# Half products of the layer 1 attention in two steps, the expert plan in two parts, row loads behind the last relay

## The chip, the cores and the metric

The kernel runs on one core of a Trainium2 chip. The metric is the device time of one execution in microseconds (us); for the kernel before, three runs are given, and their median counts.

## The reference, cut to what matters

Everything is float32. x has 8 images of 256 channels and 32 x 32 places, so 8 batches of 1024 tokens of 256 numbers.

```python
# layer 0, for each batch: xt is (1024, 256); 8 heads of 64
qkv = (xt @ w_qkv + b_qkv).reshape(B, S, 8, 192)
q, k, v = jnp.split(qkv, 3, axis=-1)
attn = softmax(jnp.einsum('bihd,bjhd->bijh', q, k) * SCALE, axis=1)   # over the queries i
res = jnp.einsum('bijh,bjhd->bihd', attn, v).reshape(B, S, 512)
t = res @ w_out + b_out + xt
# layer 1: attention of the normed tokens with themselves
n = layer_norm(t)
scores = jnp.einsum('bne,bme->bnm', jnp.einsum('bnd,ed->bne', n, W), n)
t = t + jnp.einsum('bnm,bmd->bnd', softmax(scores, axis=-1), n)
# experts: for each token the two of 8 that its router scores highest
n = layer_norm(t)
t = t + sum_e(combine_e * (gelu(n @ w1[e] + b1[e]) @ w2[e] + b2[e])) + n   # out starts from the tokens n
```

The softmax of layer 0 runs over the queries. With the keys as rows of a tile, each row is therefore a softmax of its own, and its sum divides the row of values.

## The kernel before, in words

One program goes through the batches in turn. Batch b has a layer 0, then the layer 1 attention (`attend`), then a norm, the routing and the sending of its normed tokens to rows in HBM, sorted by expert (`rows`, scattered by GpSimd). After the last layer 0 the experts of the batches sent until then run over 63 blocks of these rows; then come the attention of batch 7 and its experts, done densely. Each engine takes its instructions in the order in which the scheduler has laid them; `tc.issue_after(x)` in the code says that what follows is to be laid behind instruction x on the same engine, and makes no wait between engines.

**Layer 0** (`layer0`, from line 465) takes 4 pairs of heads g times 8 blocks of keys j, 32 steps. A step computes scores `psc` on TensorE (`score`, line 492, two tiles of 128 keys x 1024 queries), their maximum on VectorE in two halves (`first_max`, line 507; `second_max`, line 516, which writes `scrap` and the maximum), the exponential with its sum on ScalarE (`soften`, line 533), the division of the values by the sum on VectorE (`divide`, `vs`, line 549), and, two steps later, the products with the values `po` on TensorE (`gather_values`, line 569). TensorE is kept from starting a half of these products before the last half by an empty instruction, the relay (line 579): it waits for the products of one half, and those of a half in the next turn wait for it. For batch 0 the relay stands in GpSimd's queue, for the others in SyncE's.

At three steps, `PROJECT` = (0,3), (1,1), (2,1), sixteen products of the projection of the next pair (`pqk`, line 371, 7.06 us together) fill TensorE, while the maxima of that step have been taken. Work for VectorE is laid into this time: the counts and places of the routing of the batch before (`share`), and at (2,1) the residual (`residual`, lines 454 to 462): two transposes of the input tile on VectorE and an addition of the bias on GpSimd.

In the last layer 0 (b = 7), at (2,1) and behind the residual, stands the plan (`plan`, lines 1092 to 1166). It is some thirty small VectorE instructions that turn the counts of rows for each expert into a list: for each block of 256 rows the expert that it belongs to, its first row (`row_at`) and the place of the expert's weights (`w_at`). Two kinds of instruction wait for the list. GpSimd gathers the weights of the first blocks (`weights`, line 1222), by `w_at`. SyncE loads rows (`fetch`): it reads `row_at` into a register (`value_load`, line 1234) and issues the four loads of a block (`xr`, line 1239); before the change the first of them is laid behind nothing. VectorE then transposes the rows (`xb`, line 1245), and the first products of the experts (`ph`, line 1256), gelu (`hb`, line 1266) and second products (`pe`, line 1282) follow.

After the last `po`, layer 0 ends with the output product `pr` (line 666, 64 matmuls), which VectorE adds to the residual.

**Layer 1** (`attend`, from line 673) norms the tokens, projects them (`px`, line 703) and computes scores of 1024 x 1024 as four pairs of blocks of 128 rows. A pair (`Pair`) makes its two blocks in seven half products (line 753) instead of eight, from sums of halves that VectorE makes beforehand (t1 to t4, s1 to s4). The product x lies in one bank of an accumulator and grows: ScalarE copies it after its first product (line 741, `first`), after its second (line 745, `second`) and after its third (line 748), into tiles `home` (their name in the trace is `home` or `spare`); VectorE adds other products to these copies, taking the minimum on the way (`add`, line 763). `rest` makes the last two products and the exponentials (lines 786, 795, 803). A block is then transposed for the product with the tokens: block 0 and block 7 on TensorE (`turn_now`, line 842), the others (`turn`) by one VectorE transpose of squares (line 824) and sixteen moves of squares (line 835), eight of them copies on ScalarE, eight DMAs of SyncE. `mix` multiplies the turned block with the tokens (`py`, line 852).

The order of it is written by hand at the end of `attend`. In before, `Pair(k)` makes five of the seven products at once, and `rest` the other two.

Of the kernel before, what the change touches and what calls it, by code (L numbers as in the profile page):

```python
# [12 lines left out]
AF = mybir.ActivationFunctionType  # L13
ALU = mybir.AluOpType
# [5 lines left out]
def kernel(  # L20
# [23 lines left out]
    nc = tc.nc  # L44
# [420 lines left out]
    def layer0(b, xT, begun, routing, xs):  # L465
# [91 lines left out]
        def gather_values(at, turn):  # L557
# [7 lines left out]
            for half in range(2):  # L565
                keys = ts(half, DK)
                n = (half + turn) % 2
                for h in range(2):
                    mm = nc.tensor.matmul(  # L569
                        po[n][ts(h, DK), :],  # L570
                        vss[at][keys, h, :],
                        exps[at, h][keys, ts(n, 512)],
                        start=(j == 0 and turn == 0),
                        stop=(j == NT - 1 and turn == 1),
                    )
                    if h == 0 and (j > 0 or turn > 0):
                        tc.add_manual_dep(mm.ins, past[1 - half].ins.name, BEHIND)

                turned[half] = relay.nop()  # L579
                tc.add_manual_dep(turned[half].ins, mm.ins.name, BEHIND)  # L580
# [23 lines left out]
        for at in range(last + LAG + 1):  # L604
# [38 lines left out]
            if at <= last and (g, j) in PROJECT:  # L643
# [4 lines left out]
                if (g, j) == PROJECT[-1]:  # L648
                    with tc.issue_after(firsts[at, 1].ins):
                        t1 = residual(b, xs)  # L650
                if g == 0:
                    with tc.issue_after(mm.ins), tc.issue_after(firsts[at, 1].ins):
                        counted = share(pq)
                if b == B - 1 and (g, j) == PROJECT[-1]:
                    with tc.issue_after(firsts[at, 1].ins):
                        plan(groups[0])
            elif at <= last and (g, j) > PROJECT[1]:
# [15 lines left out]
    def attend(b, t1, fill, tick=nothing):  # L673
# [51 lines left out]
        class Pair:  # L725

            def __init__(self, k):
# [8 lines left out]
                ]  # L736
                left, right = (self.ex[0][:, ts(n, HALF)] for n in range(2))
                far = self.ex[1][:, ts(1, HALF)]
                at = ts(k, P)
                self.product(self.x, a11, b11, True)  # L740
                self.first = nc.scalar.copy(left, self.x)
                second = self.product(v, a12, b21, True)
                tc.declare_no_dep(second.ins, self.first.ins, reason="the other bank")
                self.product(self.x, s2_, t2_, False)
                self.second = nc.scalar.copy(right, self.x)
                self.product(self.z, s1_, t1_, True)
                self.product(self.x, s3_, t3_, False)
                nc.scalar.copy(far, self.x)
                self.add(left, v, 3.0e38, self.low[0])
                self.add(far, self.z, 3.0e38, self.low[1])  # L750

            def product(self, to, stationary, moving, start):
# [20 lines left out]

            def rest(self):
                k = self.k
# [8 lines left out]
                def even():  # L784
                    tick(("max", 2 * k), self.add(ex0[:, HALF:], self.z, self.low[0], nmax[0]))
                    nc.scalar.activation(
                        ex0, ex0, AF.Exp, bias=nmax[0], scale=-1.0, accum_out=ssum[0][:, 0:1]
                    )

# [80 lines left out]

        pairs = [Pair(0), Pair(1)]
        first, second = pairs[0].rest()
        second = turned(*second)
        third, fourth = pairs[1].rest()
        now = turn_now(0, first[1])
        pairs.append(Pair(2))
        third = turned(*third, (pairs[2].first, pairs[2].second))
        fourth = turned(*fourth, (pairs[2].second, pairs[2].second))
        mix(0, now, *first[2:])
        mix(*second)  # L880
        fifth, sixth = pairs[2].rest()
        fifth = turned(*fifth)
        mix(*third)
        pairs.append(Pair(3))
        sixth = turned(*sixth, (pairs[3].second, pairs[3].second))
        mix(*fourth)
# [192 lines left out]
    def plan(group):  # L1079
# [6 lines left out]
        def tmp(tag, shape, dtype=F32):  # L1086
# [39 lines left out]
        nc.vector.tensor_mul(block, block, taking)  # L1126
        nc.vector.tensor_add(block, block, after)

        mine = tmp("p_mine", [nb, E])
# [13 lines left out]

        base = tmp("p_base", [E])
        nc.vector.tensor_scalar_mul(base, first, -float(BR))
        work = tmp("p_work", [nb, E])
# [6 lines left out]
        row_at = keep.tile([P, NBMAX], I32, tag="row_at", name=f"row_at_{n}", bufs=2)  # L1153
        nc.vector.tensor_copy(row_at[:, :nb], lo)
        nc.vector.tensor_scalar(hi, e_of, float(P), p_iota, ALU.mult, ALU.add)
# [7 lines left out]
        w_at = keep.tile([P, NBMAX], I32, tag="w_at", name=f"w_at_{n}", bufs=2)  # L1163
        nc.vector.tensor_copy(w_at[:, :nb], hi)

        nc.vector.tensor_scalar(
            first[:, E // 2 :], first[:, E // 2 :], left, None, ALU.subtract
        )
        group.first = first, turns
        group.where = row_at, w_at  # L1170

    def places(group):
# [40 lines left out]
    def experts(group, behind):  # L1213
# [17 lines left out]
        def fetch(b):  # L1231
            xr = rowp.tile([P, RUN, DQ], F32, tag="xr", name=f"xr_{n}_{b}")
            with tc.issue_after(loads[-1].ins) if loads else nullcontext():
                at = nc.sync.value_load(
# [404 lines left out]
```

## Time and profile before

| | us |
|---|---|
| three runs | 2336.98, 2338.59, 2345.87 |
| median | 2338.59 |
| the profiled execution | 2327.18 |
| its span on the core | 2325.2 |
| TensorE busy | 2259.1 (97%) |
| VectorE busy | 1561.8 (67%) |
| ScalarE busy | 1167.0 (50%) |
| GpSimd busy | 411.2 (18%) |
| mean granted clock of TensorE | 0.993 |

In the lines of the profile, PE is TensorE, PEld its loading of weights, DVE VectorE, ACT ScalarE, POOL GpSimd and SP SyncE; SPq is SyncE's queue, which has no work of its own but instructions and DMAs to issue. A line of a timeline has the start in the span, the duration, the engine, the line of the kernel, the operation, what it writes and reads, the shape and the number of instructions that were merged into it; in brackets stands the idle time ahead of it and what ended it. A line of waits has who waited for what: us in total, times, and the longest. The chain is the work that ended last, followed back through what released it.

Single times from the timeline, for orientation: the first and the last scores (psc) of the last layer 0 start at 1715.19 and 1863.56, of batch 6 at 1474.75 and 1610.09; the projection at its step (2,1) starts at 1794.09 and ends at 1801.15; its first `pr` starts at 1873.40. The attention of batch 1 has its first `px` at 437.38 and its last `py` at 504.05, that of batch 0 at 189.51 and 263.89, that of batch 7 at 2113.22 and 2185.99.

### The profile page before, as it was taken

The numbers are of one execution on the slowest core, as the hardware profiler recorded it, in microseconds if no ns is written. First come the engines' busy times: TensorE is split into PE (matmuls) and PEld (weight loads), VectorE is DVE, ScalarE is ACT, GpSimd is POOL, SyncE is SP. The second block draws the span as 40 slices with busy tenths as digits, with TensorE's granted clock in tenths as the row PEclk, the third lists the DMA queues.
The fourth block names the chain that finished last, engine by engine and source line by source line (L and its number), as shares of the span: only waits on it lengthen the run. The fifth ranks groups of instructions, "written<-read, shape, count | busy, mean of one in ns | idle before, by whom it ended". The sixth has DMA issues, their size and how long they took to land.

```text
span 2325.2 us, 37960 instructions
## 1 busy us (share of the span) xinstructions
PE 2259.1 (97%) x13059; PEld 1211.7 (52%) x13059; DVE 1561.8 (67%) x4029; ACT 1167.0 (50%) x2139; POOL 411.2 (18%) x392
## 2 busy tenths in 40 slices
PE   9999999999999999999999999999999899999798
PEld 3344634563356335643554355435553278886565
DVE  5775678567865786578757775677668756435765
ACT  3664466356635663656464656465546532224311
POOL 0000012000200030003000200021002124544663
PEclk9999999999999999999999999999999999999899
DMA  8995201020102010201020101100120237765664
GB/s 293 385 386 156 69 12 45 4 61 8 49 1 55 12 53 1 46 19 51 6 40 25 44 13 24 41 21 17 19 45 19 71 90 196 194 190 156 189 201 134
DMA packets 278759, 200.10 MB, mean 86 GB/s; under 512 B 189576, under 2 KB 232232, under 8 KB 276776
## 3 DMA queue, kind: packets, MB, share of 16 engines
q1 hardware_dynamic: 252472, 139.14, 21.3%
q0 software_dynamic: 25008, 58.01, 7.8%
q8 instruction: 104, 1.70, 0.3%
q10 hardware_dynamic: 1088, 0.52, 0.1%
q14 instruction: 87, 0.71, 0.1%
HBM read 108.88 MB, written 110.90 MB: 95 GB/s over the span
## 4 chain that ended last, share of the span: by engine, by line
PE 80%; ACT 6%; DVE 5%; DMA 4%; issue 3%; SPq 1%; POOL 0%; DVEq 0%; ACTq 0%; POOLq 0%
PE po L569 19%; PE psc L492 18%; PE pqk L371 7%; PE py L852 6%; PE pr L666 5%; PE pv L408 4%; PE ps L753 3%; PE ph L1256 3%; PE pe L1282 3%; PE pdy L1529 2%; PE pdh L1505 2%; PE px L703 2%; PE pqk L349 2%; DMA y<-yb 1%; ACT aT L835 1%
## 5 line engine op out<-in xcount | busy, mean ns | idle before, releaser
L533 ACT ACTIVATE ex<-psc,nmax 128x1024 f32<-128x1024 f32 x512 | 570.5, 1115 | 309.9 <-DVE scrap L516 225.9
L569 PE MATMUL po<-ex,vs 64*64 64x512 f32 x4096 | 569.6, 593 | 10.7 <-SPq L579 9.8
L492 PE MATMUL psc<-qk,qk 64*64 64x512 f32 x4096 | 573.0, 593 | 3.6 <-ACT ex L533 3.5
L516 DVE TENSOR_SCALAR_CACHE_REDUCE scrap<-psc,nmax 128x512 f32<-128x512 f32 x512 | 384.4, 751 | 166.6 <-PE psc L492 138.7
L507 DVE TENSOR_REDUCE nmax<-psc 128x1 f32<-128x512 f32 x512 | 350.3, 684 | 9.3 <-PE psc L492 9.3
L492 PEld LDWEIGHTS psc<-qk,qk 64*64 64x64 f32 x4096 | 178.7, 132 | 281.1 <-ACT ex L533 131.5
L569 PEld LDWEIGHTS po<-ex,vs 64*64 64x64 f32 x4096 | 173.1, 132 | 287.8 <-issue 84.2
L1070 POOL DMA_INDIRECT rows<-n,d_at x112 | 109.0, 973 | 663.6 <-DVE nmax L507 663.3
L997 POOL TENSOR_TENSOR t<-t,n 128x2048 f32<-128x2048 f32 x8 | 36.3, 4536 | 876.8 <-DVE n L263 876.8
L371 PE MATMUL pqk<-xT,wqkv 128*128 128x512 f32 x384 | 171.2, 599 | 0.0
L336 ACT ACTIVATE qk<-pqk,b_qks 128x512 f32<-128x512 f32 x124 | 85.6, 690 | 86.6 <-PE pqk L371 77.5
L371 PEld LDWEIGHTS pqk<-xT,wqkv 128*128 128x128 f32 x384 | 71.0, 190 | 99.9 <-issue 76.5
L1378 POOL DMA_INDIRECT yk<-y,yat x112 | 111.4, 995 | 60.4 <-issue 25.6
L408 PE MATMUL pv<-wqkv,xT 128*128 128x512 f32 x256 | 120.3, 599 | 1.6 <-DVE v L416 1.0
L852 PE MATMUL py<-n,spare 128*128 128x256 f32 x512 | 118.0, 386 | 3.9 <-DMA out_dram<-oT 3.2
L852 PEld LDWEIGHTS py<-n,spare 128*128 128x128 f32 x512 | 98.3, 193 | 29.0 <-issue 16.4
L666 PE MATMUL pr<-wo,res 128*128 128x256 f32 x512 | 111.9, 379 | 0.0
L835 ACT COPY spare<-home 32x256 f32<-32x256 f32 x256 | 103.0, 402 | 10.1 <-DVE home L824 6.7
L666 PEld LDWEIGHTS pr<-wo,res 128*128 128x128 f32 x512 | 97.2, 190 | 17.0 <-ACT res L588 3.2
L1266 ACT ACTIVATE hb<-ph,wb 128x256 f32<-128x256 f32 x96 | 40.4, 471 | 125.4 <-issue 84.0
L533 ACT ACTIVATION_READ_ACCUMULATOR ex<-psc,nmax 128x1 f32 x512 | 99.1, 194 | 0.0
L1256 PE MATMUL ph<-xb,wb 128*128 128x256 f32 x384 | 91.8, 381 | 5.7 <-DMA wb<-wpack,w_at 4.1
(256 smaller groups left out, 2889.6 us busy)
## 6 DMA issues: line engine op xcount, KB each, us to landing
rows<-wb SPq DMA_DIRECT2D x7, 8192.0 KB
xr<-rows SPq DMA_DIRECT2D x252, 64.0 KB
y<-yb POOLq DMA_DIRECT2D x63, 256.0 KB, 2.6
xs<-in_x_dram SPq DMA_DIRECT2D x64, 128.0 KB
spare<-home SPq DMA_DIRECT2D x256, 32.0 KB
out_dram<-oT SPq DMA_DIRECT2D x60, 128.0 KB
xT<-in_x_dram SPq DMA_DIRECT2D x7, 1024.0 KB
sums<-t SPq DMA_DIRECT2D x7, 1024.0 KB
```

The costliest lines, as they stand in the source:

```text
L371: mm = nc.tensor.matmul(pq[:, ts(n, 512)], wqkv[:, cc, t, ts(g, P)], xT[:, cc, ts(n, 512)], start=(cc == 0), stop=(cc == NCC - 1),)
L408: nc.tensor.matmul(pv, self.xT[:, cc, ts(i, P)], wqkv[:, cc, 2, :], start=(cc == 0), stop=(cc == NCC - 1),)
L492: mm = nc.tensor.matmul(pss[at, h][ts(c, DK), ts(n, 512)], k[r, j * P + c * DK : j * P + (c + 1) * DK], q[r, ts(n, 512)], start=True, stop ...
L507: firsts[at, h] = nc.vector.tensor_reduce(nmax, pss[at, h][:, ts(0, 512)], AX.X, ALU.max, negate=True)
L516: seconds[h] = nc.vector.tensor_scalar(scrap, pss[at, h][:, ts(1, 512)], -1.0, nmaxes[at, h], ALU.mult, ALU.min, accum_out=nmax,)
L533: nc.scalar.activation(ex, pss.pop((at, h)), AF.Exp, bias=nmaxes.pop((at, h)), scale=1.0, accum_out=sums[at][:, h : h + 1],)
L569: mm = nc.tensor.matmul(po[n][ts(h, DK), :], vss[at][keys, h, :], exps[at, h][keys, ts(n, 512)], start=(j == 0 and turn == 0), stop=(j == ...
L666: nc.tensor.matmul(pr[:, :C], res[:, g, ts(i, P)], wo[:, g, :], start=(g == 0), stop=(g == NPAIR - 1))
L835: move(to[ts(k, SQ), a], since[ts(a, SQ), k])
L852: evicted["mixed"] = nc.tensor.matmul(py[:, :D], aT[m], n1[:, m, :], start=(m == 0), stop=(m == NT - 1))
L1256: last = nc.tensor.matmul(ph[:, ts(fc, BR)], wb[:, dc * FF + fc * P : dc * FF + (fc + 1) * P], xb[:, dc, :], start=(dc == 0), stop=(dc == ...
L1378: ins = nc.gpsimd.indirect_dma_start(out=self.slot(at)[:, k, :], out_offset=None, in_=self.group.y[:, :], in_offset=bass.IndirectOffsetOnAxis(
```

## The change

It has three parts.

1. **Half products in two steps a pair.** `Pair(k)` now makes three products (x's first, v and z's first), and its new method `middle` the second and third of x, with their copies. The first two pairs do both at once. Pair 2's `middle` is laid behind the first mix, and pair 3's behind the third; pair 3 itself starts before the third mix. The moves of block 5 (`fifth`) and block 6 (`sixth`) are laid behind copies of pair 3, those of `third` and `fourth` as before behind copies of pair 2. The exponential of the first block is laid behind the third copy of pair 1 (`rest(pairs[1].third)`).
2. **The plan in two parts.** `plan` becomes a generator. Its first part, up to the block numbers, `base` and the rest of `first`, runs at step (1,1) of the last layer 0; its second part, up to `row_at` and `w_at`, at (2,1), ahead of the residual, which is laid behind it.
3. **Row loads behind the last relay.** The first `fetch` is laid behind the last relay of the last layer 0 (`evicted["relayed"]`) on SyncE, so that no row load stands between relays.

```diff
--- before.py
+++ after.py
@@ -576,7 +576,7 @@
                     if h == 0 and (j > 0 or turn > 0):
                         tc.add_manual_dep(mm.ins, past[1 - half].ins.name, BEHIND)
 
-                turned[half] = relay.nop()
+                turned[half] = evicted["relayed"] = relay.nop()
                 tc.add_manual_dep(turned[half].ins, mm.ins.name, BEHIND)
             if turn == 0:
                 return mm
@@ -646,14 +646,19 @@
                     pair, pq, mm = project_pair(b, xT, g + 1)
                 qks.append(pair)
                 if (g, j) == PROJECT[-1]:
-                    with tc.issue_after(firsts[at, 1].ins):
+                    ahead = firsts[at, 1]
+                    if b == B - 1:
+                        with tc.issue_after(ahead.ins):
+                            ahead = next(planning)
+                    with tc.issue_after(ahead.ins):
                         t1 = residual(b, xs)
                 if g == 0:
                     with tc.issue_after(mm.ins), tc.issue_after(firsts[at, 1].ins):
                         counted = share(pq)
-                if b == B - 1 and (g, j) == PROJECT[-1]:
+                if b == B - 1 and (g, j) == PROJECT[1]:
+                    planning = plan(groups[0])
                     with tc.issue_after(firsts[at, 1].ins):
-                        plan(groups[0])
+                        next(planning)
             elif at <= last and (g, j) > PROJECT[1]:
                 share(firsts[at, 1])
         for _ in routing:
@@ -734,20 +739,23 @@
                     small.tile([P, 1], F32, tag=f"nlow{h}", name=f"nlow_{b}_{k}_{h}")
                     for h in range(2)
                 ]
-                left, right = (self.ex[0][:, ts(n, HALF)] for n in range(2))
-                far = self.ex[1][:, ts(1, HALF)]
-                at = ts(k, P)
+                self.left = self.ex[0][:, :HALF]
                 self.product(self.x, a11, b11, True)
-                self.first = nc.scalar.copy(left, self.x)
+                self.first = nc.scalar.copy(self.left, self.x)
                 second = self.product(v, a12, b21, True)
                 tc.declare_no_dep(second.ins, self.first.ins, reason="the other bank")
-                self.product(self.x, s2_, t2_, False)
-                self.second = nc.scalar.copy(right, self.x)
                 self.product(self.z, s1_, t1_, True)
+                self.add(self.left, v, 3.0e38, self.low[0])
+
+            def middle(self, behind=None):
+                far = self.ex[1][:, HALF:]
+                with tc.issue_after(behind.ins) if behind else nullcontext():
+                    self.product(self.x, s2_, t2_, False)
+                self.second = nc.scalar.copy(self.ex[0][:, HALF:], self.x)
                 self.product(self.x, s3_, t3_, False)
-                nc.scalar.copy(far, self.x)
-                self.add(left, v, 3.0e38, self.low[0])
+                self.third = nc.scalar.copy(far, self.x)
                 self.add(far, self.z, 3.0e38, self.low[1])
+                return self
 
             def product(self, to, stationary, moving, start):
                 return nc.tensor.matmul(
@@ -771,7 +779,7 @@
                     accum_out=to,
                 )
 
-            def rest(self):
+            def rest(self, behind=None):
                 k = self.k
                 self.product(self.z, s4_, b22, False)
                 self.product(self.x, a22, t4_, False)
@@ -783,9 +791,10 @@
 
                 def even():
                     tick(("max", 2 * k), self.add(ex0[:, HALF:], self.z, self.low[0], nmax[0]))
-                    nc.scalar.activation(
-                        ex0, ex0, AF.Exp, bias=nmax[0], scale=-1.0, accum_out=ssum[0][:, 0:1]
-                    )
+                    with tc.issue_after(behind.ins) if behind else nullcontext():
+                        nc.scalar.activation(
+                            ex0, ex0, AF.Exp, bias=nmax[0], scale=-1.0, accum_out=ssum[0][:, 0:1]
+                        )
 
                 def odd():
                     last = nc.vector.tensor_scalar(
@@ -868,21 +877,23 @@
         def turned(at, ex, ssum, more, behind=None):
             return at, turn(at, ex, behind), ssum, more
 
-        pairs = [Pair(0), Pair(1)]
-        first, second = pairs[0].rest()
+        pairs = [Pair(0).middle(), Pair(1).middle()]
+        first, second = pairs[0].rest(pairs[1].third)
         second = turned(*second)
         third, fourth = pairs[1].rest()
         now = turn_now(0, first[1])
         pairs.append(Pair(2))
+        mix(0, now, *first[2:])
+        pairs[2].middle(evicted["mixed"])
         third = turned(*third, (pairs[2].first, pairs[2].second))
         fourth = turned(*fourth, (pairs[2].second, pairs[2].second))
-        mix(0, now, *first[2:])
         mix(*second)
         fifth, sixth = pairs[2].rest()
-        fifth = turned(*fifth)
+        pairs.append(Pair(3))
         mix(*third)
-        pairs.append(Pair(3))
-        sixth = turned(*sixth, (pairs[3].second, pairs[3].second))
+        pairs[3].middle()
+        fifth = turned(*fifth, (pairs[3].second, pairs[3].second))
+        sixth = turned(*sixth, (pairs[3].third, pairs[3].third))
         mix(*fourth)
         seventh, eighth = pairs[3].rest()
         seventh = turned(*seventh)
@@ -1125,6 +1136,13 @@
         nc.vector.tensor_sub(block, block, after)
         nc.vector.tensor_mul(block, block, taking)
         nc.vector.tensor_add(block, block, after)
+        base = tmp("p_base", [E])
+        nc.vector.tensor_scalar_mul(base, first, -float(BR))
+        nc.vector.tensor_scalar(
+            first[:, E // 2 :], first[:, E // 2 :], left, None, ALU.subtract
+        )
+        group.first = first, turns
+        yield
 
         mine = tmp("p_mine", [nb, E])
         of = block.unsqueeze(2).to_broadcast([P, nb, E])
@@ -1141,8 +1159,6 @@
             ALU.is_equal,
         )
 
-        base = tmp("p_base", [E])
-        nc.vector.tensor_scalar_mul(base, first, -float(BR))
         work = tmp("p_work", [nb, E])
         lo, hi = tmp("p_lo", [nb]), tmp("p_hi", [nb])
         nc.vector.tensor_mul(work, mine, base.unsqueeze(1).to_broadcast([P, nb, E]))
@@ -1151,7 +1167,7 @@
         nc.vector.tensor_scalar_min(lo, lo, float(cap - BR))
         nc.vector.scalar_tensor_tensor(lo, e_of, float(cap), lo, ALU.mult, ALU.add)
         row_at = keep.tile([P, NBMAX], I32, tag="row_at", name=f"row_at_{n}", bufs=2)
-        nc.vector.tensor_copy(row_at[:, :nb], lo)
+        placed = nc.vector.tensor_copy(row_at[:, :nb], lo)
         nc.vector.tensor_scalar(hi, e_of, float(P), p_iota, ALU.mult, ALU.add)
         same = tmp("p_same", [nb])
         nc.vector.tensor_tensor(
@@ -1161,13 +1177,10 @@
             hi[:, NXB:], same[:, NXB:], float(E * P), hi[:, NXB:], ALU.mult, ALU.add
         )
         w_at = keep.tile([P, NBMAX], I32, tag="w_at", name=f"w_at_{n}", bufs=2)
-        nc.vector.tensor_copy(w_at[:, :nb], hi)
-
-        nc.vector.tensor_scalar(
-            first[:, E // 2 :], first[:, E // 2 :], left, None, ALU.subtract
-        )
-        group.first = first, turns
+        with tc.issue_after(placed.ins):
+            copied = nc.vector.tensor_copy(w_at[:, :nb], hi)
         group.where = row_at, w_at
+        yield copied
 
     def places(group):
 
@@ -1230,7 +1243,7 @@
 
         def fetch(b):
             xr = rowp.tile([P, RUN, DQ], F32, tag="xr", name=f"xr_{n}_{b}")
-            with tc.issue_after(loads[-1].ins) if loads else nullcontext():
+            with tc.issue_after((loads[-1] if loads else evicted["relayed"]).ins):
                 at = nc.sync.value_load(
                     row_at[0:1, b : b + 1], min_val=0, max_val=E * group.cap - BR
                 )
```

## The prediction, made before the changed kernel was run

> **What bounds the kernel now.** I read the page first, then the chain of waits by line, then the timelines of the two stages that the change touches.
>
> ```profile
> PE 2259.1 (97%) x13059; PEld 1211.7 (52%) x13059; DVE 1561.8 (67%) x4029; ACT 1167.0 (50%) x2139; POOL 411.2 (18%) x392
> PE 80%; ACT 6%; DVE 5%; DMA 4%; issue 3%; SPq 1%; POOL 0%; DVEq 0%; ACTq 0%; POOLq 0%
> ```
>
> TensorE is busy for 2259.1 of 2325.2 us and holds 80% of the chain. The change doesn't remove matmuls, so it can win only from the 66 us of gaps, and lose by opening new ones. The gaps that it touches lie in two places. The first is the last layer 0 (TensorE's timeline):
>
> ```profile
> 1801.15 1.09 PE L492 MATMUL psc<-qk,qk 64*64 64x512 f32 x8
> 1802.06 1.04 PE L569 MATMUL po<-ex,vs 64*64 64x512 f32 x8
> 1802.92 1.04 PE L492 MATMUL psc<-qk,qk 64*64 64x512 f32 x8
> 1810.90 1.98 PE L569 MATMUL po<-ex,vs 64*64 64x512 f32 x8 [6.94 <-SPq L579]
> 1843.53 1.09 PE L569 MATMUL po<-ex,vs 64*64 64x512 f32 x8 [1.72 <-SPq L579]
> 1848.46 1.09 PE L569 MATMUL po<-ex,vs 64*64 64x512 f32 x8 [1.15 <-SPq L579]
> ```
>
> Value products (po) wait for the relay, an empty instruction on SyncE. VectorE's and GpSimd's timelines, and SyncE's waits, tell why:
>
> ```profile
> 1795.02 2.36 DVE L458 STREAM_TRANSPOSE t<-xs 128x1024 f32<-128x1024 f32 x2
> 1797.30 0.14 DVE L1092 TENSOR_SCALAR p_edge<-b_iota 128x28 f32<-128x28 f32 x1
> 1798.32 3.95 DVE L1102 TENSOR_TENSOR_SCAN p_ends<-ones,p_blocks 128x8 f32<-128x8 f32 x1
> 1808.90 0.74 DVE L516 TENSOR_SCALAR_CACHE_REDUCE scrap<-psc,nmax 128x512 f32<-128x512 f32 x1
> ```
> ```profile
> 1797.52 4.72 POOL L462 TENSOR_TENSOR t<-t,b_o 128x2048 f32<-128x2048 f32 x1 [1.17 <-issue]
> ```
> ```profile
> SPq L1234 <- DVE nmax L507: 7.2, 1, 7.2
> ```
> ```profile
> SPq L1239 <- DMA rows<-n,d_at: 3.5, 1, 3.5
> ```
>
> The reader is to see the plan on VectorE from 1797.30 to 1808.90, ahead of the score maximum that the next exponential needs, and row loads on SyncE that hold the relays behind them for 7.2 and 3.5 us. The maximum should have come at 1802.31 (batch 6's came at 1561.91, and the batches stand 240.40 apart). The price: from first to last score (psc) this layer 0 takes 148.37 us, those of batches 1 to 6 135.30 to 135.57 (mean 135.45). The excess is 12.9 us.
>
> The second place is the attention of layer 1 (TensorE, batch 1):
>
> ```profile
> 464.91 1.12 PE L753 MATMUL ps<-mixes 128*128 128x512 f32 x2 [0.47 <-ACT home L741]
> 467.18 1.12 PE L753 MATMUL ps<-mixes,xa 128*128 128x512 f32 x2 [0.28 <-ACT home L745]
> 481.69 1.12 PE L753 MATMUL ps<-mixes,xa 128*128 128x512 f32 x2 [1.33 <-ACT home L745]
> ```
>
> Batches 1 to 6 each have these three gaps, 2.08 us in sum. Batch 0 has 5.8 (2.09 and 1.98 the largest).
>
> **What the Trainium skill says.** "SBUF — State Buffer", section "SBUF: two separate sides": VectorE and GpSimd share a port pair under an exclusive lock; a VectorE operation with two SBUF inputs waits out a GpSimd operation that reads SBUF. The trace agrees: the 8-column scan above took 3.95 us under GpSimd's add, and a 64-column scan elsewhere 0.29. "PSUM — Partial Sum Buffer", section "Engine vs sequencer instructions": the queues of ScalarE, VectorE and GpSimd are strict FIFO. The trace shows the maximum standing behind the plan. "TensorE: Matmul & The Clock Gate", Part 1: after an idle window of some 3.4 us the array runs at half clock. The trace agrees: after the gap of 6.94, eight products took 1.98 us instead of 1.04.
>
> **The change, part by part.**
>
> Plan, part 1 (edge to first-left), goes to step (1,1). Without the lock the plan's own time is about 11.5 − 3.95 + 0.17 = 7.7, with overlaps 8.2; by its rows part 1 is 3.4 and part 2 4.85. VectorE's window at (1,1) is 7.30 us (1760.32 to 1767.62), of which routing counts take 3.9. That leaves 3.40: part 1 just fits, cost 0 to 0.2. The projection's 7.06 us of TensorE hides it; without that cover it would cost its 3.4.
>
> Plan, part 2, goes ahead of the residual's transposes at (2,1): 1795.02 + 4.85 + 2.36 = 1802.2, against the maximum's 1802.31. The old lateness of 6.6 us goes. What is late next is GpSimd's add. It followed the transposes at 1797.5, in the projection's cover; now it comes after them at 1802.2, and behind two weight gathers (wb, 1.02 each, also freed early by the plan), so about 1802.7 to 1807.3. In this time VectorE must do vs (L549, two SBUF inputs), which comes 2.44 after the maximum: 1804.8. Locked out until 1807.3 it is 2.5 late; po needs it within about 0.2. Bound: 0 (no lock) to 4.6 (the add starts just ahead of vs and no earlier step was late). I take 2.3. The maxima read PSUM and one SBUF scalar and don't wait.
>
> Row loads go behind the last relay. The value load and 18 xr issues leave the relays' way, so the gaps of 6.94, 1.72, 1.15 and the slack lost around them go. Sum for the layer: 12.9 − 2.3 = **−10.6** (−8.4 to −12.9).
>
> The loads now come late. SyncE needs 2.7 us a block of rows (1876.59 to 1879.32 where nothing holds it) and about 2 us to land, so the first block arrives 4.5 to 5 us after the last po. Behind po stands the output product pr, 13.8 us, which covers it; without this cover experts would wait 5. The first expert products (ph, 2.15 us) stood among the last po, with a gap of 1.47; they now come after pr, and the gelu ahead of the first pe stands behind a table load of 1.28, an estimated gap of 0.9. From last score to first pe it took 25.05; now 4.75 (as batches 1 to 6, their filler taken off) + 13.8 + 3.5 + 0.9 = 23.0, and up to 1 more for copies of rows on VectorE. I take **−1.0** (−2 to +0.5).
>
> Half products: of each pair three products start at once, and two more (`middle`) later, after the mix of the pair before. Same number of matmuls and copies. Their cost is the order on ScalarE, where eight moves of 0.41 make a block of 3.3. Walking batch 1's queues with the durations above: start +0.13 (the first exponential now stands behind a third copy); the gaps of 0.47, 0.28 and 1.33 become about 1.0 (pair 2's third product: a copy of pair 3 stands ahead of its own on ScalarE and waits for a VectorE transpose) and 0.84 (pair 3). The middle runs 0.4 us earlier. But the end isn't set there: exponential of block 6, transpose, DMAs of the moves, last py. That exponential now stands behind eight moves where it stood behind four and a copy: 488.3 against 487.96. So a batch ends +0.3 later, not earlier (−0.4 to +0.6). I take 0.35; six of them **+2.1**.
>
> Batch 7's attention has other things beside it. Its gap of 1.09 for a moved block covers the new early wait; pair 3's last product waits about 3.2 for a copy behind eight moves; the end, set by DMAs on SyncE, comes 0.8 earlier. A wait of 3.2 may bring the half clock (up to 1.7 by the page's 3.4 us, an estimate): **−0.3** (−2 to +2).
>
> Batch 0: pair 3's first copy stood behind ten moves (the 2.09) and now stands ahead of them. After those gaps sixteen py took 5.65 instead of 3.62. From px to the last py it takes 74.38, others 66.7, so up to 5 us could go, but the end is bound as in the others: **−1.7** (−5 to +1).
>
> Sum −10.6 − 1.0 + 2.1 − 0.3 − 1.7 = **−11.5** us. The profiled execution took 2327.18 (span 2325.2), so 2315.7, a ratio of 0.9951; on the median of 2338.59 (the profiled one was 0.5% below it) that is 2327. A measurement of this kernel tells about 0.5% (11.7 us) from no change.
>
> **Rivals.**
> - The lock doesn't bite and batch 0's half clock goes: another −2.3 and −2.5, so −16.3: 2322. For it: VectorE may be late or early by a us; against: the 3.95 scan.
> - Half products lose more than the walk says, 1.2 in each of eight: −11.6 + 9.6 = −2: 2336. For it: the end of each is bound by ScalarE and moves, not by TensorE's gaps.
> - Slower than before: the same block of eight moves stands ahead of a needed copy and all that is behind it moves by nearly its whole 3.3, say 3.0, in all eight: −11.6 + 24 = +12.4: 2351. It breaks even at 1.45 an attention. Against: each stage has slack of 1 to 2 us on ScalarE (idle 0.84, 0.97 and 2.37 in batch 1).
> - The plan moves but stays late: at (1,1) only 3.40 is free, and a GpSimd operation that reads SBUF there would lengthen the scan by up to 3.7, and the seam waits 3 for rows: −4: 2334.5.
>
> **How the numbers follow.** The sum above 0.45 (its own range 2323 to 2331), no lock 0.25, half products losing 0.14, slower 0.08, plan late 0.08. The range 2320 to 2337 leaves out the slower case and the low end of the second. Faster by over 0.5% (below 2326.9): half of the first and nearly all of the second, 0.46; slower 0.10 (the slower case and a little of the rest); within 0.5%: 0.44.
>
> **What would show it.** Right: the last layer 0 near 138 us from first to last score; one gap of about 2 us at a po after the second projection, with vs or GpSimd's add behind it; no SPq L579 gaps; no row loads until the last po; 66 to 67.3 us from px to last py in batches 1 to 6. Wrong: a new gap at (1,1), gaps of over 2 us at ph or pe at the seam, or attentions over 68 us.

## The result, and the profile after

| | us |
|---|---|
| the changed kernel, six runs | 2325.02 to 2329.83, median 2327.43 |
| the kernel before, six runs in the same sessions | 2336.98 to 2346.86, median 2342.85 |
| ratio | 0.9941, 95% interval 0.9929 to 0.9952 |
| both again on another chip: after 2315.93, before 2328.23 | 0.9947 (0.9934 to 0.9961) |
| the changed kernel's profiled execution | 2328.95, span 2327.1 |

The forecast was 2327 and a ratio of 0.9951. Chips differ here: the kernel before takes 2326 to 2331 us on two of them (the first kind below) and 2337 to 2347 on others (the second). The profile of before that the prediction reads, 2327.18, is like those of the first kind, while its three times are like those of the second. So only times of one session are set against each other, and stages only within one kind.

The last layer 0 after, TensorE's timeline around the projection at (2,1): no relay ends a wait any more, and one gap is left.

```profile
1801.42 1.04 PE L492 MATMUL psc<-qk,qk 64*64 64x512 f32 x8
1804.08 1.09 PE L569 MATMUL po<-ex,vs 64*64 64x512 f32 x8 [1.63 <-DVE vs L549]
```

VectorE's timeline around it, and GpSimd's:

```profile
1791.80 0.67 DVE L1149 TENSOR_TENSOR p_mine<-p_block,p_ends 128x504 f32<-128x504 f32 x1
...
1796.59 2.37 DVE L458 STREAM_TRANSPOSE t<-xs 128x1024 f32<-128x1024 f32 x2
1799.09 0.75 DVE L516 TENSOR_SCALAR_CACHE_REDUCE scrap<-psc,nmax 128x512 f32<-128x512 f32 x1
...
1801.64 2.38 DVE L549 TENSOR_TENSOR vs<-v,rs 128x128 f32<-128x128 f32 x1
```
```profile
1799.34 4.53 POOL L462 TENSOR_TENSOR t<-t,b_o 128x2048 f32<-128x2048 f32 x1
```

Part 2 of the plan takes 4.79 us (1791.80 to 1796.59), the transposes follow, and the maximum comes at once, not 6.6 us late. What is late now is vs: it takes 2.38 us instead of 0.29, beside GpSimd's addition, which runs from 1799.34 to 1803.87. From first to last score this layer 0 takes 137.57 us, before 148.37.

The attention of batch 1 after, TensorE, then ScalarE:

```profile
463.60 1.12 PE L761 MATMUL ps<-mixes,xa 128*128 128x512 f32 x2 [0.33 <-ACT home L754]
475.79 1.12 PE L761 MATMUL ps<-mixes,xa 128*128 128x512 f32 x2 [0.73 <-ACT home L754]
492.26 3.69 PE L861 MATMUL py<-n,spare 128*128 128x256 f32 x16 [0.67 <-DVE t L870]
```
```profile
475.15 0.58 ACT L754 COPY home<-ps 128x512 f32<-128x512 f32 x1 [2.68 <-PE ps L761]
475.63 1.66 ACT L844 COPY home<-home 32x256 f32<-32x256 f32 x4
477.31 0.58 ACT L756 COPY home<-ps 128x512 f32<-128x512 f32 x1
477.92 1.65 ACT L844 COPY home<-home 32x256 f32<-32x256 f32 x4
479.60 3.30 ACT L844 COPY spare<-home 32x256 f32<-32x256 f32 x8
482.93 1.15 ACT L795 ACTIVATE home<-home,nmax 128x1024 f32<-128x1024 f32 x1
```

The gaps in the middle are smaller than before (1.25 us with one of 0.19, where they were 2.08), but a new one of 0.67 stands ahead of the last but one py. It is the product of the block that the code calls `seventh`. The prediction counts blocks from 0 and calls it block 6; "block 5 (`fifth`)" and "block 6 (`sixth`)" in the section on the change count from 1. The exponential of `seventh` (482.93) now starts straight behind sixteen moves with a copy among them, twelve of them behind that copy. Ahead of the moves and of the copy at 475.15, ScalarE was idle for 2.68 us. From the first px to the last py it takes 66.91 us instead of 66.67.

By stages, in the profiles of before and of the changed kernel's repetition (`after_again` below), both like the first kind (an attention is measured from its first px to its last py):

| stage | before | after | measured | forecast |
|---|---|---|---|---|
| attention, batch 0 | 74.38 | 69.05 | -5.3 | -1.7 |
| attention, batches 1 to 6 | 400.97 | 402.59 | +1.6 | +2.1 |
| last layer 0, first to last score | 148.37 | 137.59 | -10.8 | -10.6 |
| last score to batch 7's px (seam, expert blocks) | 249.66 | 251.40 | +1.7 | -1.0 |
| batch 7's px to the end | 211.98 | 215.71 | +3.7 | -0.3 |
| span | 2325.2 | 2316.6 | -8.6 | -11.5 |

These stages sum to -9.1. The medians on the chip of `after_again` differ by 12.3. Single executions of one kernel spread over 4 to 5 us there, and the profiled one of `after_again`, 2318.43, is the slowest of its five.

### The profile page after: what moved, and what is told of

Its sections match the earlier page's. It is cut to its first block, busy times and chain, and to the rows that moved or that the text cites. A ratio compares the mean times of both kernels' runs of the same rounds, so it can differ in the third digit from the quotient of the medians.

```text
span 2327.1 us, 37989 instructions
## 1 busy us (share of the span) xinstructions
PE 2261.6 (97%) x13059; PEld 1216.1 (52%) x13059; DVE 1554.5 (67%) x4029; ACT 1163.0 (50%) x2138; POOL 410.7 (18%) x392
## 4 chain that ended last, share of the span: by engine, by line
PE 80%; ACT 5%; DVE 4%; issue 4%; DMA 3%; POOL 3%; SPq 1%; another core or an unknown queue 0%; DVEq 0%; ACTq 0%; POOLq 0%
PE po L569 19%; PE psc L492 19%; PE py L861 7%; PE pqk L371 7%; PE pr L671 5%; PE pv L408 4%; PE ps L761 4%; PE ph L1269 3%; PE pe L1295 3%; PE px L708 2%; POOL yk L1391 2%; PE pqk L349 2%; PE ps1z L761 2%; DMA y<-yb 1%; ACT aT L844 1%
## 5 line engine op out<-in xcount | busy, mean ns | idle before, releaser
L870 DVE SCALAR_TENSOR_TENSOR t<-py,rs,t 128x256 f32<-128x256 f32 x64 | 30.5, 476 | 98.0 <-PE py L861 85.3
```

## Experiments

**First question: which part brings the gain, and why do the two first profiles (span 2325.2 before, 2327.1 after) not show it?** Four kernels on one chip: each half of the change alone, the changed kernel with batch 7's attention as it was, and the kernel before again.

`half_only`: before, with the `attend` of the changed kernel and no other edit.

> The half products in two steps alone, the plan and the row loads as in the kernel before. My theory by the two traces: batch 0's attention 5.3 us shorter, batches 1 to 6 1.7 us longer together, batch 7's attention longer (11.1 us in the one profile). If that profile is typical, this is 7 to 8 us slower than before, ratio about 1.003. Rival (batch 7's attention in the kernel before is as slow in its other executions as in the changed kernel's profile, the profiled one being a lucky one): 2 to 4 us faster than before, ratio about 0.9985.

Measured: ratio 0.9994 (0.9985 to 1.0003). No gain that can be told. Neither number held; the rival's was the nearer one.

`plan_rows`: the changed kernel with the `attend` of before.

> The plan in two parts and the row loads behind the last relay alone, attention as before. My theory: 11 to 12 us faster than before (last layer 0 near 137.6 us from first to last score), ratio 0.995. Rival (these parts shift the last stages so that batch 7's attention gets slower, whatever the order of its half products): only 0 to 4 us faster, ratio 0.998 to 1.0, and its profile shows batch 7's attention above 78 us from px to last py.

Measured: 0.9956 (0.9939 to 0.9972), that is -10 us of 2340.51; last layer 0 at 137.39. The gain is that of the plan and the row loads. Batch 7's attention took 79.11 us, as the rival had it, but it took 79.40 in the kernel before on this chip too (`before_again` below), so these parts are not the cause.

`last_whole`: batch 7's attention alone goes back.

```diff
-        t2 = attend(b, t1, fill, others.tick)
+        t2 = attend_whole(b, t1, fill, others.tick)   # the attend of before
```

> The changed kernel, with batch 7's attention alone in the order of before (five of seven half products at once). My theory that the two steps cost batch 7 its 11 us: 2316 to 2320, ratio to before 0.990, batch 7's attention back at 72 to 74 us. Rival (the 11 us are the state of the DMA queues and of the clock in this stage, not the order): as the changed kernel, ratio 0.994, and batch 7's attention stays above 78 us.

Measured: 0.9948 (0.993 to 0.9965), batch 7's attention 80.83 us. My theory fell: the order is not what made most of the 83.85 us that batch 7's attention took in the first profile of after. From its px to the end it is 225.0 us with the old order and 227.4 in that profile, so some 2 us may be the order's.

`before_again`: no edit.

> The kernel before once more, for a second profile. Its profiled execution of 2327.18 us lies 10 to 20 us below each of its six timed ones. If batch 7's attention varies from one execution to the next, its second profile is longer by 10 us or more there, and as before everywhere else. If the profiled execution is faster as such, the second one is near 2327 again.

Measured: 2342.05 us, the profile's span 2340.0. Batch 7's attention takes 79.40 us (72.77 in the first profile), from its px to the end 225.0 us (212.0). The two profiles of before differ by 14.8 us, 13.0 of them in this last stage; the expert blocks ahead of it take 4.4 us more as well, and two other stages 2.6 less. TensorE and VectorE in the last stage:

```profile
2172.03 5.39 PE L852 MATMUL py<-n,home 128*128 128x256 f32 x16 [5.60 <-DVE t L861]
```
```profile
2171.49 0.48 DVE L861 SCALAR_TENSOR_TENSOR t<-py,rs,t 128x256 f32<-128x256 f32 x1 [4.91 <-remote]
```

The fourth py of this attention ended at 2163.28 by the timeline, yet VectorE, which adds it to t, starts only at 2171.49. It waits for TensorE's semaphore, the counter by which TensorE tells what it has finished, and that got three updates together at 2171.47 to 2171.55. The trace of this execution holds 2648 updates of the semaphore where TensorE's instructions make 2676; the first profile of before holds 2677. The missing ones all lie behind the last score: 10 of 148 in the expert blocks, 8 of 36 in batch 7's attention, 10 of 59 behind it. The changed kernel shows the same: 2653 of 2685 in the first profile, 2687 in that of `after_again`, on a chip of the first kind. What delays TensorE's signals on some chips stays open. It strikes both kernels; the ratio is nearly the same with it (0.9941) and without (0.9947).

**Second question: within the plan and the row loads, what is each worth, and what is the gap of 1.63?** One profiled execution each, on a chip of the first kind, where the kernel before took 2325.79 to 2330.76 us.

`plan_only`: `plan_rows` with the old place of the row loads.

```diff
-            with tc.issue_after((loads[-1] if loads else evicted["relayed"]).ins):
+            with tc.issue_after(loads[-1].ins) if loads else nullcontext():
```

> The plan in two parts alone: row loads stand between the relays as before, attention as before. My theory that plan and row loads are two separate costs: the gap of 6.9 us is gone, the two relay gaps further on (1.7 and 1.2 us) stay, the last layer 0 takes 140 to 143 us from first to last score (148 before, 137.6 with both). Rival (the plan alone made the loss, the row loads only stood in a queue that was not needed): 137.6. Other rival (row loads hold the relays whenever the plan ends): above 145.

Measured: 140.59 us from first to last score (2318.09 in all), and the two later gaps are there on TensorE:

```profile
1805.74 1.09 PE L569 MATMUL po<-ex,vs 64*64 64x512 f32 x8 [1.64 <-DVE vs L549]
1834.42 1.09 PE L569 MATMUL po<-ex,vs 64*64 64x512 f32 x8 [1.73 <-SPq L579]
1839.12 1.09 PE L569 MATMUL po<-ex,vs 64*64 64x512 f32 x8 [0.91 <-SPq L579]
```

`rows_only`: before, with the opposite edit.

> The row loads behind the last relay alone: the plan whole at its old place, behind the residual, attention as before. My theory: the maximum still waits for the plan on VectorE until 1808.9, so a gap of 5 to 6.5 us stays after the second projection, now with VectorE or ScalarE behind it instead of SyncE's relay, and the later two go: the last layer 0 at 143 to 145 us. Rival (SyncE's relay was the wait that counted): 138 to 140.

Measured: 143.82 us, and TensorE waits at the same place for another engine, ScalarE, which in turn waits for VectorE's maximum behind the plan:

```profile
1810.23 1.98 PE L492 MATMUL psc<-qk,qk 64*64 64x512 f32 x8 [6.20 <-ACT ex L533]
```
```profile
1808.97 1.11 ACT L533 ACTIVATE ex<-psc,nmax 128x1024 f32<-128x1024 f32 x1 [7.81 <-DVE scrap L516]
```

In this layer 0 the row loads alone save 4.6 us (148.37 to 143.82), the plan alone 7.8 (to 140.59), together 10.8. These sizes are rough: the kernel before took 146.87 in `before_again`, where the last relay wait (1.15 in the first profile) was absent, and 147.89 in `half_only`, which has the same layer 0. The wait of 6.94 that the profile put down to SyncE's relay had two causes that ended at nearly the same time: with the relay free it is 6.20 and ends at VectorE's plan, by way of the exponential. Whoever had moved only the loads, because the profile names SPq, would have got less than half of the layer's gain. In its whole time `rows_only` shows none, 2326.88 us, since its seam and expert blocks took 6.6 us more than before; with one execution, why is not known.

`add_late`: the changed kernel; the last bias addition moves from GpSimd to VectorE, behind the last division.

```diff
-        nc.gpsimd.tensor_add(t1, t1, b_o.unsqueeze(1).to_broadcast([P, NT, C]))
+        if b < B - 1:
+            nc.gpsimd.tensor_add(t1, t1, b_o.unsqueeze(1).to_broadcast([P, NT, C]))
...
                 evicted["divided"] = divide(last)
+                if b == B - 1:
+                    with tc.issue_after(evicted["divided"].ins):
+                        nc.vector.tensor_add(t1, t1, b_o.unsqueeze(1).to_broadcast([P, NT, C]))
```

> The changed kernel, with the addition of the bias to the last residual taken from GpSimd and done on VectorE behind the last division, where VectorE is idle for 5 us. My theory (GpSimd's addition locks vs out): vs at that place takes 0.29 us instead of 2.38, the gap of 1.63 us at po goes, the last layer 0 takes 135.7 to 136.2 us instead of 137.57. Rival (vs is late because part 2 of the plan makes VectorE late): gap and 137.6 stay.

Measured: 135.52 us (2315.98 in all), no gap at that po. VectorE's timeline:

```profile
1801.30 0.29 DVE L550 TENSOR_TENSOR vs<-v,rs 128x128 f32<-128x128 f32 x1
...
1850.49 2.28 DVE L638 TENSOR_TENSOR t<-t,b_o 128x2048 f32<-128x2048 f32 x1
1855.76 0.42 DVE L678 TENSOR_TENSOR t<-pr,t 128x256 f32<-128x256 f32 x1 [2.98 <-PE pr L675]
```

vs is back at 0.29 with the plan where it was, so GpSimd's addition was the cause and not a late plan. The 2.28 us of the moved addition lie in idle time of VectorE, of which 2.98 is still left.

**Third question: what sets the end of an attention?** `fifth_early`, the changed kernel with one word changed:

```diff
-        fifth = turned(*fifth, (pairs[3].second, pairs[3].second))
+        fifth = turned(*fifth, (pairs[3].first, pairs[3].second))
```

> The changed kernel, with the first half of the moves of block 5 laid behind pair 3's first copy instead of its second. In batch 1 of the changed kernel ScalarE idles 2.68 us ahead of that second copy, and the exponential of block 6 stands behind twelve moves after it. My theory (these moves, by way of that exponential, set the end of each attention): the exponential starts 0.9 us earlier, where the maximum now holds it, the gap of 0.67 us at the last but one py goes, and batches 1 to 6 take 66.2 to 66.4 us instead of 66.9 to 67.7; 3 to 5 us less in all, ratio to before 0.992. Rival (the end is set by DMAs on SyncE or by another wait): 66.9 as in the changed kernel, ratio 0.994.

Measured: ratio 0.993 (0.991 to 0.995), batches 1 to 6 at 65.97 to 66.58 us, 0.9 us less each. ScalarE in batch 1:

```profile
472.55 1.66 ACT L844 COPY home<-home 32x256 f32<-32x256 f32 x4
475.23 0.59 ACT L754 COPY home<-ps 128x512 f32<-128x512 f32 x1 [1.02 <-PE ps L761]
...
482.13 1.15 ACT L795 ACTIVATE home<-home,nmax 128x1024 f32<-128x1024 f32 x1 [0.70 <-DVE nmax L771]
```

Four moves now fill the idle time (2.68 becomes 1.02 behind them), and the exponential starts 0.9 us earlier after the attention's first px, with 0.70 us of idle ahead of it: the maximum holds it now, as forecast. The gap ahead of py is gone on TensorE, where the last but one product follows the one ahead of it without a wait:

```profile
488.05 7.11 PE L861 MATMUL py<-n,spare 128*128 128x256 f32 x32
```

The attention (65.99 us in batch 1) is shorter than before the change too (66.67).

**Last question: does it hold on one chip, and what is the best version?** Three kernels, five executions each, on one chip of the first kind. `after_again` is the changed kernel, `both` has the edits of `add_late` and `fifth_early`, `best` also has batch 7's attention as before.

> The changed kernel once more, against the kernel before on one and the same chip. My theory: 10 to 14 us faster, ratio 0.9940 to 0.9957 on either kind of chip: layer 0 of batch 7 -10.8, batch 0's attention -4 to -5, batches 1 to 6 +1.7, batch 7's attention and the end together +2.5 to +4 (in the profiles of chip 6 and chip 7). Rival (the first comparison, 0.9941, came from the chip as much as from the change): ratio 0.997 or more on this chip.

Measured: 0.9947 (0.9934 to 0.9961), 2315.93 us against 2328.23.

> The changed kernel with both mends: half of block 5's moves earlier, and the last residual's addition on VectorE behind the last division. Theory (each acts alone, in another stage): -5.5 (six attentions at 66.0 instead of 66.9) and -2.0 (last layer 0 at 135.5 instead of 137.6) against the changed kernel, so 7 to 8 us less than it, ratio to before 0.991. Rival (gains at TensorE are given back where DMAs set the pace in the last stages): within 3 us of the changed kernel.

Measured: 0.9918 (0.9904 to 0.9931), 2308.20 us, 7.7 less than the changed kernel on the same chip. In its profile the six attentions take 65.96 to 66.40 us and the last layer 0 135.55.

> As the run before, and batch 7's attention in the order of before (five of seven half products at once). Theory (the two steps cost batch 7 some 3 us, by the profiles of two kinds of chip): 2 to 4 us less than the run before, ratio to before 0.9895. Rival (batch 7's attention and the end are paced by gathers and moves, not by that order): the same as the run before within 1.5 us.

Measured: 0.9911 (0.9897 to 0.9924), 2307.43 us, 0.8 less than `both`: the rival's number in the time. In the profiles, batch 7's px to the end takes 212.34 us instead of 214.03, although `best` has a wait of 3.57 us at the last but one py that the other profiles of the old order on chips of the first kind don't have. `best` is the fastest version tried, but against `both` this isn't settled.

## Why the prediction was right, point by point

**Last layer 0**: right in place, mechanism and size (-10.8 for -10.6; against `before_again` -9.3). Shown: the plan and the loads are two causes (`plan_only`, `rows_only`), and the new cost is vs under GpSimd's addition (`add_late`). The forecast for it was 2.3; moving the addition away gained 2.05. The projection starts 3.2 us earlier after; shifted by this, the addition was forecast at 1799.5 to 1804.1 and ran from 1799.34 to 1803.87. Part 1 at (1,1) fits better than I had counted: 2.38 us of VectorE's window are left where I had none. Its small instructions were laid in turn with those of the counts, and both together took 4.9 us, where the prediction had added 3.4 and 3.9: laid in turn, one starts every 0.13 us or so, where the counts alone, before, started every 0.26.

**The seam and the expert blocks**: forecast -1.0, measured +1.7, outside -2 to +0.5 and on the other side. From last score to first pe it is 24.67 us in the first profile (25.05 before), so the seam itself gives -0.4: the term counted 23.0 and up to 1 more, and left out two gaps that products of the experts had filled, 1.00 at the last po (behind vs) and 0.68 at the first pr. The rest lies in the expert blocks, and there +1.7 can't be told from nothing: over all profiles this stage takes 249.66 to 254.11 us with the row loads early and 248.71 to 256.25 with them late.

**Batches 1 to 6**: +1.6 for +2.1, and the chain named (exponential of block 6, its moves, the py after) was shown by `fifth_early`. The prediction had this exponential behind eight moves; behind the last copy it is twelve, and they were late because ScalarE idled for an earlier copy. The two middle gaps, forecast at about 1.0 and 0.84, were 0.33 and 0.73.

**Batch 0**: -5.3 for -1.7, beyond its range by a little. The mechanism was right and the size off: I held the gain back because the end is bound as in the others. In fact, of the waits of 2.09 and 1.98 the first is gone, with one of 0.57 ahead of another product, and the second is 1.56; the half clock that had followed them is gone as well. Before, then in the first profile of after, where the sixteen py behind the second wait run at full speed:

```profile
229.50 2.08 PE L753 MATMUL ps<-mixes,xa 128*128 128x512 f32 x2 [1.98 <-ACT home L745]
231.36 5.65 PE L852 MATMUL py<-n,aT 128*128 128x256 f32 x16
```

```profile
227.01 1.12 PE L761 MATMUL ps<-mixes,xa 128*128 128x512 f32 x2 [1.56 <-ACT home L754]
227.97 3.62 PE L861 MATMUL py<-n,aT 128*128 128x256 f32 x16
```

In the five profiles of kernels with the old order this attention took 72.8 to 74.5 us, each with half clock in it; in the eight with the new one it took 69.04 or 69.05, without.

**Batch 7's attention and the end**: forecast -0.3, measured +3.7. That the "gap of 1.09 for a moved block covers the new early wait" held: pair 2 waits 1.05 and 0.68, where before 0.48, 0.28 and the 1.09 stood. Two steps failed. The first: the wait of about 3.2 was put at pair 3's last product, which waits only 0.68; 2.33 lie at its second. I walked ScalarE's queue and not VectorE's, where batch 7, unlike the others, has additions of gathered rows (o) between the half products' additions. In `after_again`, TensorE and VectorE:

```profile
2141.45 1.83 PE L761 MATMUL ps<-mixes 128*128 128x512 f32 x2 [2.33 <-DVE nlow L771]
2143.06 4.65 PE L861 MATMUL py<-n,spare 128*128 128x256 f32 x16
```
```profile
2136.99 2.06 DVE L1413 SCALAR_TENSOR_TENSOR o<-yk,gate,o 128x256 f32<-128x256 f32 x5
2138.97 0.73 DVE L771 CUSTOM_DVE_ANT_0 home<-home,ps1z,nlow 128x512 f32<-128x512 f32 x1
...
2140.71 0.68 DVE L771 CUSTOM_DVE_ANT_0 home<-home,ps 128x512 f32<-128x512 f32 x1
```

Pair 3's second product waits until VectorE has added v to the first copy, and this addition (2140.71) stands behind the o additions and a maximum. Before, that product didn't wait in the first profile, and 0.77 us for ScalarE's copy in `before_again`. The second step that failed: "the end, set by DMAs on SyncE, comes 0.8 earlier". The py that waits for these DMAs, before and in `after_again`:

```profile
2172.80 6.09 PE L852 MATMUL py<-n,spare 128*128 128x256 f32 x16 [3.19 <-DMA out_dram<-oT]
```
```profile
2163.65 6.35 PE L861 MATMUL py<-n,spare 128*128 128x256 f32 x16 [3.30 <-DMA out_dram<-oT]
```

It starts 59.58 us behind the first px before and 62.76 after, with nearly the same wait ahead of it, so nothing that was lost earlier is made up there. Of these 3.2 us, 1.4 are waits ahead of it (5.59 against 4.19 in sum) and 1.7 the half clock that follows the 2.33, which slows the product to 1.83 us and the sixteen py behind it to 4.65, where they took 1.12 and 3.62 in `both`. The prediction had named this half clock as possible, with the same 1.7. `both` has the same waits without it, and its attention takes 75.24 us instead of 76.98. What remains, +1.0 behind that py and -0.5 after the attention, isn't explained by a run.

The profiles fall into two groups by the order of batch 7's attention. On chips of the first kind its px to the end takes 210.4 to 212.4 us in four kernels with the old order and 214.1 to 216.0 in four with the new one; on the second kind it is 225.0 to 225.5 in three and 227.4 and 228.2 in two. These kernels differ in other parts too. The one pair that was timed side by side and differs in this order alone, `both` and `best`, shows 0.8, within its spread.

So the sum was right partly because errors cancelled: batch 0 gave 3.6 us more than forecast, the seam, the expert blocks and the last stage took 6.7 more. That the number itself, 2327, was met within 1 us is luck. It was counted from a median of 2338.59; over six runs that median is 2342.85, so the difference measured there is 15.4 us and not 11.5, and on the chip of `after_again` it is 12.3.

**The rivals.** That the lock doesn't bite was wrong (`add_late`); the other half of that rival, that batch 0's half clock goes, came true. Half products as a loss of 1.2 in each attention: batches 1 to 6 lost 0.3 each, and with batch 0 and batch 7 the half products end at 0.9994. Slower than before, by 3.0 in each attention: nothing of that size outside batch 7. That the plan stays late was wrong: the maximum came on time.

## What to carry to other kernels

A wait that the profile gives to one queue may hide a second that ends just before it: undo each by itself before counting the gain. When work is moved out of one engine's way, look for what used to run under its cover (here GpSimd's addition) and now meets a VectorE instruction with two SBUF inputs (here vs). Where an in-order queue idles for a copy while moves stand behind it, lay some of the moves ahead of the copy. In batches 1 to 6 one word took 0.9 us off each attention, where the whole reordering had added 0.3. When an order is walked through by hand, walk every queue that takes part: in batch 7 the wait came from VectorE's, which had been left out.

## What the runs showed of the hardware

- vs, on VectorE with two SBUF inputs, took 0.29 us alone and 2.38 in the changed kernel and 2.39 in `plan_only`, where GpSimd's addition ran beside it; in both it ended 0.15 us behind that addition. Reductions and maxima from PSUM ran beside the same addition at their usual 0.69 and 0.75 us.
- The half clock did not need one wait of some 3.4 us, as the prediction had it. In batch 0 it came before the change, at waits of 2.09 and 1.98 us with 1.1 us of work between them, and not after it, at waits of 0.57 and 1.56. In batch 7, `after_again`, `add_late`, `fifth_early` and `both` have the same waits (1.05, 0.68, 2.33, 0.68); in `after_again` and `fifth_early` it came behind the third, in `add_late` behind the second, in `both` not at all. The clock records of the thirteen profiles point to why. The half clock starts on a grid that runs through the whole execution in steps of 3.413 us (the starts at 228.64, 1809.02 and 2170.83 in before stand 463 and 106 steps apart). From 200 us on, 64 steps that began at full clock had TensorE idle for more than half of them, and 60 of these were followed by half clock; of 7885 others 10 were, nine of them between 2203 and 2228. The waits named here fill 0.68 of a step in `after_again` and `fifth_early`, 0.51 in `add_late` and at most 0.42 in `both`, so it matters where in the grid a wait falls.
- On chips of the second kind, updates of TensorE's semaphore came late in the last stage (by 8.2 us in `before_again`) and several at once, and each of the five traces there lacks 28 to 37 of them; on the first kind none is missing by this count. The stage took 13 us longer in `before_again`; the cause wasn't found.
